# Two of eight expert groups summed on TensorE instead of scattered to memory, in a fused four-block transformer kernel

## The chip, the cores and the metric

One core of a Trainium2 chip runs the whole program. The metric is device time in microseconds (us) of that core for one execution, as the median of several runs. The core has five engines that run side by side, each from its own queue in order: TensorE (PE in the profile; its weight loads are PEld) for matmuls, VectorE (DVE) and ScalarE (ACT) for element work, GpSimd (POOL), which here mostly issues indirect DMAs, and SyncE (SP), which issues the plain DMAs. Engines wait for each other through semaphores. SBUF is the on-chip memory; PSUM is where TensorE writes its products.

## The reference

The reference passes 4096 tokens of 128 features through twelve sublayers: four blocks, each of a half-weighted feed-forward, an attention and the same feed-forward again. The change is in the two feed-forwards of block 1, a mixture of experts:

```python
x = x + 0.5 * _L1_ffn_ref(_layernorm(x), ...)
x = x + _L1_attn_ref(_layernorm(x), ...)
x = x + 0.5 * _L1_ffn_ref(_layernorm(x), ...)

def _moe_forward(x, router_w, w_gate, w_up, w_down, ws_gate_up, ws_down):
    probs = softmax(x @ router_w.T)                  # 64 experts
    topk_w, topk_ids = top_k(probs, 8)
    topk_w = topk_w / sum(topk_w)
    ...                                              # pos: how many earlier tokens chose that expert
    valid = pos < 64                                 # 64 places per expert
    xb = ...                                         # (64 experts, 64 places, 128)
    h = silu(xb @ w_gate) * (xb @ w_up)              # 96 hidden
    y = h @ w_down
    routed = segment_sum(y * topk_w * valid, token)
    shared = silu(x @ ws_gate) * (x @ ws_up) @ ws_down
    return routed + shared
```

The expert takes the first 64 tokens that chose it. With 64 x 64 = 4096 places and 8 choices a token, 512 tokens at the least are needed to fill all places; for the given input the first 1024 tokens fill them. Later tokens get the shared expert alone.

## The kernel before

**Layout.** `x` holds all tokens in SBUF as 32 blocks of 128 tokens; a piece is four blocks (512 tokens), so there are eight pieces. `xn` is the normalised x and `xnT` its transpose, which the matmuls read. `norm_piece(c)` does one piece's layernorm: statistics and an inverse root on VectorE (L305 to L319), then four scalings on ScalarE (L328). `turn_piece(c)` transposes it: four matmuls into `ln_tp` and a copy by ScalarE (L336, L337). All transposes share one PSUM pool, `pst`, with two buffers ("tp"): whoever takes a buffer waits, in the order of the program, until the user before the last has been read.

**Order.** `pin` (L240) chains instructions of one engine in the order in which the program writes them. So the queue of each engine is set by hand in the expert loop; outside of it a scheduler places them.

**Routing.** `ffn1(call, normed)` (L963) handles `FIRST` = 8 blocks (two pieces) in general. `routing` computes logits, a softmax, the best eight of 64 (L1002 to L1031). `slots` (L1038) finds for every expert its first 64 tokens: eight rounds of MAX8 and MATCH_REPLACE8 on VectorE, transposes of the result into lists (L937 to L943), then `idx` and `idy`, the row numbers for the gathers and scatters (L1064, L1065). `f_cp` and `more` (L1080, L1081) count the places that are still empty. The shared expert of the first two pieces follows in the text: `shared_up` (L979), a gate product `sgp`, an up product `sup`, silu and their product `sh`; `shared_down` (L991), a product `yp` (in the PSUM bank of `sgp`) added to x (L996). Then x of these pieces is stored to memory as accumulator `acc[0]` (L234). There are four accumulators in memory in all; the other three start at zero.

Every engine then reads `more` and branches (L1121): only if places were empty does `general()` handle all tokens. For this input the branch is always taken past it.

**Experts.** The 64 experts go in eight groups of eight. For group g: `fetch` (L1134, four indirect gathers on GpSimd), `turn` (L1145), `gates` (L1156, sixteen matmuls, silu on ScalarE L1158), `product` (L1163, `hh` on VectorE), `down` (L1172, products `y`; L1188, VectorE multiplies by the routing weight into `ys`; L1192, four indirect scatter-adds on GpSimd into the accumulators). Sixteen matmuls on a constant (`idle`, L258) go ahead of the first group. In the same loop run the shared expert of the other six pieces, the load of the weights two groups ahead (L1114, L1116), and the layernorm of pieces for what follows. In call 0 that is attention; in call 1 (`normed`) it is block 2, whose experts choose tokens: `pick` (L1426: logits `f_lp`, L1436, L1447) and `best` (L1452: four rounds of MAX8, FIND_INDEX8 and MATCH_REPLACE8 per piece, L1458 to L1464, split in two halves of two rounds).

**End.** A second branch on `more` (L1254) guards the return of the later pieces. In call 0 attention then reads the accumulators of the first two pieces into SBUF (`returned` L1359, with L1363 and L1367) and sums them with three VectorE adds a piece (`summed`, L1370). It begins with other pieces: `project` (a_zp L1278, a_nm L1293). In call 1 `gather_acc` (L946) does the same at once: x from acc[0] (L952), six loads of the other accumulators (L955), six adds (L956), and then `choose` normalises, picks and searches for these two pieces.

Of the kernel before, what the change touches and what calls it, by code (L numbers as in the profile page):

```python
# [9 lines left out]
F32 = mybir.dt.float32  # L10
# [21 lines left out]
NS0 = NB0 * B0 // P  # L32

E1, K1, F1, CAP1 = 64, 8, 96, 64
FIRST = 8
XW = D + E1
GE1 = 8
# [34 lines left out]
def macaron_kernel(ctx: ExitStack, tc: tile.TileContext, I: dict, out: bass.AP):  # L72
# [146 lines left out]
    xl_dram = dram.tile([T + PAD, XW], F32, name="xl_dram")  # L219

    acc_two = [dram.tile([2 * (T + PAD), D], F32, name=f"acc{n}") for n in range(NACC // 2)]
    acc = [a[h * (T + PAD) : (h + 1) * (T + PAD), :] for a in acc_two for h in range(2)]
    SP.dma_start(out=xw_dram[T:, :], in_=zeros[:, :XW])
    SP.dma_start(out=xn_dram[T:, :], in_=zeros[:, :D])
# [114 lines left out]
    def tok(j):  # L339
        return xnT[:, j * P : (j + 1) * P]  # L340
# [618 lines left out]
    piece_order = [FIRST // 4, FIRST // 4 + 1, *range(FIRST // 4), *range(FIRST // 4 + 2, NT // 4)]  # L959
    begun = piece_order[:2]  # L960


    def ffn1(call, normed):  # L963
        pinned.clear()
# [7 lines left out]
        with tc.tile_pool(name=f"f1r{call}", bufs=1) as rp, tc.tile_pool(name=f"f1w{call}", bufs=2) as wp, tc.tile_pool(  # L972
            name=f"f1t{call}", bufs=2
        ) as tp2:
            idx = rp.tile([P, E1 // 2], I32, name="f1_idx")
            idy = rp.tile([P, E1 // 2], I32, name="f1_idy")
            more = rp.tile([1, 1], I32, name="f1_more")
# [60 lines left out]
            def slots(key, n, key_pool):  # L1038

                keyT = key_pool.tile([P, n * P], F32, tag="keyT", name="f1_keyT")  # L1040
                for c in range(0, n, 4):
                    tp = pst.tile([P, 512], F32, tag="tp", name="f1_ktp")
                    for i in range(4):
                        PE.transpose(
                            tp[:, i * P : (i + 1) * P], key[:, c + i, :, :].rearrange("p h e -> p (h e)"), ident
                        )
                    S.copy(keyT[:, c * P : (c + 4) * P], tp)
                first = key_pool.tile([P, CAP1], F32, tag="first", name="f1_first")
                for r in range(CAP1 // 8):
# [12 lines left out]
                for h in range(2):  # L1062
                    rows = slice(h * CAP1, (h + 1) * CAP1)
                    V.tensor_scalar(idx[rows, :], empty[rows, h::2], float(T), None, ALU.add)  # L1064
                    V.tensor_scalar(idy[rows, :], empty[rows, h::2], float(T + h * (T + PAD)), None, ALU.add)  # L1065
                return slot

            with tc.tile_pool(name=f"f1p{call}", bufs=2, space=PSUM) as pr, tc.tile_pool(name=f"f1k{call}", bufs=1) as key_pool:
# [53 lines left out]
                general()  # L1122

            pinned.clear()
            with tc.tile_pool(name=f"f1h{call}", bufs=1, space=PSUM) as ph:
                n, groups, others = GE1 // 2, E1 // GE1, NT // 4 - FIRST // 4
                xgs, turned, hidden, w = {}, {}, {}, early
# [36 lines left out]

                def down(g):
                    wd, (hh, _) = w[g][1], hidden.pop(g)
                    y = ph.tile([P, n, D], F32, tag="y", name="f1_y", bufs=2)
                    for i in range(n):
                        for h in range(2):
                            e = 2 * i + h  # L1170
                            pin(
                                PE.matmul(  # L1172
                                    y[h * CAP1 : (h + 1) * CAP1, i, :],
                                    hh[:, e * CAP1 : (e + 1) * CAP1],
                                    wd[:, e, :],
                                    start=True,
                                    stop=True,
                                    skip_group_check=True,
                                )
                            )  # L1180

                    flat = xgs.pop(g).rearrange("p e w -> p (e w)")
                    ys = tp2.tile([P, n, D], F32, tag="ys", name="f1_ys", bufs=2)
                    for h in range(2):
                        rows = slice(h * CAP1, (h + 1) * CAP1)
                        w0 = D + g * GE1 + h
                        wcol = flat[rows, w0 : w0 + (n - 1) * (XW + 2) + 1 : XW + 2]
                        pin(V.tensor_tensor(ys[rows, :, :], y[rows, :, :], bc(wcol, 2, D), ALU.mult))  # L1188
                    for i in range(n):
                        e = g * n + i  # L1190
                        pin(
                            G.indirect_dma_start(  # L1192
                                out=acc_two[e % 2],
                                out_offset=bass.IndirectOffsetOnAxis(ap=idy[:, e : e + 1], axis=0),
                                in_=ys[:, i, :],
                                in_offset=None,
                                compute_op=ALU.add,
                            )
                        )
# [12 lines left out]
                for g in range(groups):  # L1212
# [41 lines left out]
            with tc.If(rv > 0):  # L1254
                gather_acc(acc, FIRST, NT, add=True)
                if normed:
                    choose(range(FIRST // 4, NT // 4))
                else:
                    for c in begun:
                        norm_piece(c)  # L1260
                        turn_piece(c)
            if normed:
                gather_acc(acc, 0, FIRST, n=4, bufs=6)
                choose(range(FIRST // 4))


    def attn1():

        scale = float(DH) ** -0.5 / D
        with tc.tile_pool(name="a1", bufs=3) as ap, tc.tile_pool(name="a1a", bufs=2, space=PSUM) as pa, tc.tile_pool(  # L1270
# [88 lines left out]
            def returned(c):  # L1359

                rows = slice(4 * c * P, (4 * c + 4) * P)
                xc = x[:, 4 * c : 4 * c + 4, :]
                SP.dma_start(out=xc, in_=acc[0][rows, :].rearrange("(j p) d -> p j d", p=P))  # L1363
                parts[c] = []
                for a in acc[1:]:
                    t = ap.tile([P, 4, D], F32, tag="acc", name="acc_t", bufs=6)
                    SP.dma_start(out=t, in_=a[rows, :].rearrange("(j p) d -> p j d", p=P))  # L1367
                    parts[c].append(t)

            def summed(c):  # L1370
                xc = x[:, 4 * c : 4 * c + 4, :]
                for t in parts.pop(c, []):
                    pin(V.tensor_tensor(xc, xc, t, ALU.add))

            pinned.clear()
            parts = {}
# [9 lines left out]
            for s in range(BATCH + 7):  # L1386
# [12 lines left out]
                    if p < pieces:  # L1399
                        turn_piece(piece_order[p])  # L1400
                if s in ahead:
                    summed(piece_order[ahead[s]])
# [890 lines left out]
```

## Time and profile before

| | |
|---|---|
| median of 8 runs | 2882.48 us (2873.9 to 2893.54) |
| profiled execution, its own time | 2885.66 us |
| span in its trace | 2884.0 us |
| mean granted TensorE clock | 0.859 of full |
| busy: PE / DVE / ACT / POOL | 2343.1 / 1490.7 / 1059.5 / 768.5 us |
| PE share of the chain that ended last | 32% |
| call 0: gates of group 0 to first a_nm of attention | 720.79 to 825.86 us |
| call 1: gates of group 0 to the first scaling after the return | 981.89 to 1134.28 us |
| scatter-adds of both calls (L1192) | 64, mean 1570 ns |

The times are from the start of the span. The granted clock is the share of its full rate at which TensorE was let run in a stretch of time. "SPq", "DVEq" or "PEq" is the part of an engine that handles waits, branches and DMA issues; idle time "<-DVEq L1121" is idle time that ended when that engine had passed the branch of line 1121.

### The profile page before, as it was taken

The page shows a single profiled execution, that of the slowest core. Times are in us where ns is not written, and L with a number is a line of the kernel's source. Part 1 is how long each engine was busy: PE and PEld are TensorE (multiplying, and loading weights), DVE is VectorE, ACT ScalarE, POOL GpSimd, SP SyncE. Part 2 cuts the span into 40 slices and gives each one's busy share as a digit, 9 for nine tenths or more (in the row PEclk, how much of TensorE's full clock was granted, in tenths as well). Part 3 has the DMA queues.
Part 4 walks back from the last instruction along what each step waited for, and adds up shares of the span by engine and source line. Part 5 has one row for each costly group of instructions (what it writes and reads, how often), then busy time and mean ns, then how long its engine had stood idle before and what let it go on. Part 6 is the DMA issues. An engine that isn't in the chain of part 4 may idle for free. (4 is left out here: it accounts for less than half of the span.)

```text
span 2884.0 us, 45798 instructions
## 1 busy us (share of the span) xinstructions
PE 2343.1 (81%) x16869; PEld 1720.2 (60%) x16869; DVE 1490.7 (52%) x4388; ACT 1059.5 (37%) x2388; POOL 768.5 (27%) x695
## 2 busy tenths in 40 slices
PE   6986887993866573477999993786999899999999
PEld 5873555792655452355666662554777655557777
DVE  5446565445557566423345566224555666645553
ACT  1322221231234221243444431443444355663443
POOL 1650000561730352476000102872111100012111
PEclk9997887996779665677999995658999799999999
DMA  5861231563530445356000003552000012220000
GB/s 153 274 163 48 77 104 60 168 180 91 148 69 8 122 106 143 76 148 150 23 5 8 5 8 96 137 140 67 1 1 1 10 49 64 64 66 7 8 8 11
DMA packets 207909, 221.14 MB, mean 77 GB/s; under 512 B 46265, under 2 KB 172938, under 8 KB 204306
## 3 DMA queue, kind: packets, MB, share of 16 engines
q1 hardware_dynamic: 171066, 179.80, 20.3%
q0 software_dynamic: 36608, 38.31, 7.5%
q8 instruction: 136, 2.23, 0.3%
q14 instruction: 99, 0.81, 0.1%
HBM read 145.88 MB, written 63.50 MB: 73 GB/s over the span
## 5 line engine op out<-in xcount | busy, mean ns | idle before, releaser
L328 ACT ACTIVATE xn<-x,ln_less,ln_r 128x128 f32<-128x128 f32 x288 | 118.6, 482 | 380.4 <-DVE ln_less L319 374.6
L871 DVE TENSOR_REDUCE a_nm<-a_s 128x4 f32<-128x1024 f32 x128 | 156.4, 1224 | 102.1 <-PE a_t L867 90.4
L515 PE MATMUL f_h<-f_xsT,f_w 128*128 128x256 f32 x736 | 183.3, 393 | 1.5 <-DVE f_xsT L504 1.4
L1667 PE MATMUL f_h<-f_xgT,f_w 128*128 128x128 f32 x768 | 152.8, 360 | 36.8 <-DVE f_xgT L1661 36.8
L875 ACT ACTIVATE a_e<-a_t 128x512 f32<-128x512 f32 x256 | 139.0, 594 | 98.9 <-PE a_t L867 98.9
L1671 ACT ACTIVATE f_hs<-f_h,w_f_b 128x128 f32<-128x128 f32 x384 | 109.5, 369 | 172.1 <-PE f_h L1667 168.8
L867 PE MATMUL a_t<-a_q,a_k 32*128 32x256 f32 x1024 | 168.3, 412 | 3.5 <-ACT a_e L875 3.3
L1667 PEld LDWEIGHTS f_h<-f_xgT,f_w 128*128 128x128 f32 x768 | 129.7, 255 | 60.8 <-DVE f_xgT L1661 60.8
L1702 POOL DMA_INDIRECT acc<-f_ys,f_idx x96 | 151.9, 1582 | 49.8 <-DVE f_ys L1697 29.3
L518 DVE SCALAR_TENSOR_TENSOR f_hs<-f_h,f_b1s,f_sg 128x256 f32<-128x256 f32 x184 | 88.8, 484 | 141.7 <-ACT f_sg L517 141.7
L867 PE MATMUL a_s<-a_k,a_q 32*128 32x256 f32 x1024 | 155.5, 431 | 2.3 <-DVE a_nm L871 1.6
L517 ACT ACTIVATE f_sg<-f_h,f_b1s 128x256 f32<-128x256 f32 x184 | 87.1, 474 | 170.5 <-PE f_h L515 169.6
L515 PEld LDWEIGHTS f_h<-f_xsT,f_w 128*128 128x128 f32 x736 | 133.7, 196 | 24.0 <-issue 7.6
L336 PE MATMUL ln_tp<-ident,xn 128*128 128x128 f32 x288 | 64.1, 337 | 97.5 <-ACT xn L328 97.2
L1697 DVE TENSOR_SCALAR f_ys<-f_up,f_xg,f_share 128x128 f32<-128x128 f32 x96 | 39.3, 410 | 187.9 <-PE f_up L1694 162.8
L2089 ACT ACTIVATE f_nh<-f_c,w_f_sh 128x256 f32<-128x256 f32 x192 | 87.0, 500 | 127.7 <-DVE f_c L2108 103.2
L489 POOL DMA_INDIRECT f_xs<-xn_dram,f_src x92 | 91.0, 989 | 132.8 <-DVE f_own L458 57.9
L2036 POOL TENSOR_TENSOR f_t<-f_nh 128x512 f32<-128x512 f32 x16 | 20.4, 1273 | 380.7 <-PE f_m L2070 361.1
L867 PEld LDWEIGHTS a_s<-a_k,a_q 32*128 32x128 f32 x1024 | 90.9, 198 | 47.3 <-issue 34.0
L1192 POOL DMA_INDIRECT acc<-f_ys,f_idy x64 | 100.5, 1570 | 64.5 <-DVE f_ys L1188 37.6
L867 PEld LDWEIGHTS a_t<-a_q,a_k 32*128 32x128 f32 x1024 | 104.4, 189 | 17.2 <-ACT a_e L875 12.6
L336 PEld LDWEIGHTS ln_tp<-ident,xn 128*128 128x128 f32 x288 | 40.3, 162 | 124.6 <-ACT xn L328 110.8
(455 smaller groups left out, 5563.1 us busy)
## 6 DMA issues: line engine op xcount, KB each, us to landing
f_w<-in_f_w SPq DMA_DIRECT2D x24, 1024.0 KB
f_w<-in_f_w SPq DMA_DIRECT2D x46, 512.0 KB
f_w<-in_f_w SPq DMA_DIRECT2D x70, 256.0 KB
a_ud<-a_u SPq DMA_DIRECT2D x32, 512.0 KB
f_wgu<-in_f_wgu SPq DMA_DIRECT2D x16, 768.0 KB
acc<-zeros SPq DMA_DIRECT2D x14, 512.0 KB
acc_t<-acc SPq DMA_DIRECT2D x28, 256.0 KB
f_wd<-in_f_wd SPq DMA_DIRECT2D x16, 384.0 KB
```

The lines of the kernel that those rows point to most:

```text
L328: S.activation(xn[:, t0 + j, :], x[:, t0 + j, :], AF.Identity, bias=less[:, j : j + 1], scale=r[:, j : j + 1])
L336: pin(PE.transpose(tp[:, i * P : (i + 1) * P], xn[:, 4 * c + i, :], ident))
L489: G.indirect_dma_start(out=xs[:, i, :], out_offset=None, in_=xn_dram, in_offset=bass.IndirectOffsetOnAxis(ap=src[:, s : s + 1], axis=0),)
L515: pin(PE.matmul(h[:, k, :], w1[:, cc * P : (cc + 1) * P], xsT, start=True, stop=True))
L518: V.scalar_tensor_tensor(hs[:, c, :], h[:, 1, :], b1[:, b, c : c + 1], sg, ALU.add, ALU.mult)
L867: pin(PE.matmul(ps[:, c, :], sta[:, c * P : (c + 1) * P], mov, start=True, stop=True))
L871: pin(V.tensor_reduce(m, sp, AX.X, ALU.max, negate=True))
L875: pin(S.activation(e, tp, AF.Exp, scale=scale))
L1192: G.indirect_dma_start(out=acc_two[e % 2], out_offset=bass.IndirectOffsetOnAxis(ap=idy[:, e : e + 1], axis=0), in_=ys[:, i, :], in_offset= ...
L1667: pin(PE.matmul(h[:, s, :], w1[:, e % GE2, s, :], xgT, start=True, stop=True))
L1671: pin(S.activation(acts[e][:, s, :], h[:, s, :], AF.Gelu, bias=W["f2_b1"][:, col : col + 1]))
L1702: G.indirect_dma_start(out=acc2[e % 2], out_offset=bass.IndirectOffsetOnAxis(ap=idx[:, e : e + 1], axis=0), in_=ys, in_offset=None, comput ...
```

## The change

The outputs `ys` of the last two groups (6 and 7) are no longer scattered. Each group has four lists of 128 places (two experts each), eight lists in all. For each list and each of the two pieces of 512 tokens, VectorE makes a 128x512 matrix that is 1 where a place's token is the column's token (`place`), and TensorE multiplies `ys` of the list, as weights, with it, adding up over the eight lists in two PSUM banks `sums` (`put`): sixteen compares and sixteen 128x512 fp32 matmuls per call. ScalarE copies `sums` over the first 1024 columns of `xnT`, and `summed` transposes them back (four transposes a piece) and adds them to x as one more VectorE add per piece.

To find room in PSUM, `sup` of the shared expert moves from its own bank into the pool of the transposes, and `y` has one buffer instead of two. The token numbers `tokf` cost four small VectorE steps in the routing. A counting row comes from an iota on GpSimd. At most two compares of each piece are kept ready (`bufs=2`), so `place(i + 2)` waits for list i's matmul.

`returned` and `summed` move out of attention and serve both calls. In call 1 the accumulators are read within the loop, at g = 6, with three buffers instead of six, and summed ahead of the second branch. The `ys` of the two groups are also stored to `ys_dram`, so that the branch's body can scatter them when tokens behind the first 1024 have places.

```diff
+SUMMED = 2
...
+    def returned(pool, bufs=3):
+        for c in range(FIRST // 4):
+            rows = slice(4 * c * P, (4 * c + 4) * P)
+            xc = x[:, 4 * c : 4 * c + 4, :]
+            SP.dma_start(out=xc, in_=acc[0][rows, :].rearrange("(j p) d -> p j d", p=P))
+            parts[c] = []
+            for a in acc[1:]:
+                t = pool.tile([P, 4, D], F32, tag="acc", name="acc_t", bufs=bufs)
+                SP.dma_start(out=t, in_=a[rows, :].rearrange("(j p) d -> p j d", p=P))
+                parts[c].append(t)
+    def summed(c):
+        xc = x[:, 4 * c : 4 * c + 4, :]
+        for t in parts.pop(c):
+            pin(V.tensor_tensor(xc, xc, t, ALU.add))
+        tp = pst.tile([P, 512], F32, tag="tp", name="f1_stp")
+        for i in range(4):
+            pin(PE.transpose(tp[:, i * P : (i + 1) * P], tok(4 * c + i), ident))
+        pin(V.tensor_tensor(xc, xc, tp.rearrange("p (j d) -> p j d", d=D), ALU.add))
...
-                sup = pool.tile([F1, 512], F32, tag="su", name="f1_sup", bufs=1)
+                sup = pst.tile([P, 512], F32, tag="tp", name="f1_sup")[:F1, :]
...
+                    for k in range(2):
+                        late = empty[rows, E1 - 2 * tail + h :: 2]
+                        V.tensor_scalar(tokf[rows, k, :], late, float(T - 512 * k), None, ALU.add)
...
+                G.iota(count_up, pattern=[[1, 512]], base=0, channel_multiplier=0, allow_small_or_imprecise_dtypes=True)
+                sums = [ph.tile([P, 512], F32, name=f"f1_sum{k}") for k in range(2)]
+                def place(i):
+                    for k in range(2):
+                        ohs[i, k] = op.tile([P, 512], F32, tag=f"oh{k}", name="f1_oh", bufs=2)
+                        pin(V.tensor_scalar(ohs[i, k], count_up, tokf[:, k, i : i + 1], None, ALU.is_equal))
+                def put(g):
+                    ys = yss.pop(g)
+                    for j in range(n):
+                        i = (g - groups + SUMMED) * n + j
+                        for k in range(2):
+                            pin(PE.matmul(sums[k], ys[:, j, :], ohs.pop((i, k)),
+                                start=i == 0, stop=i == tail - 1, skip_group_check=True))
+                        if i + 2 < tail:
+                            place(i + 2)
...
-                    y = ph.tile([P, n, D], F32, tag="y", name="f1_y", bufs=2)
+                    y = ph.tile([P, n, D], F32, tag="y", name="f1_y", bufs=1)
...
+                    if g >= groups - SUMMED:
+                        late = (g - groups + SUMMED) * n * P
+                        SP.dma_start(out=ys_dram[late : late + n * P, :]..., in_=ys)
+                        yss[g] = ys
+                        return
                     for i in range(n):
                         e = g * n + i
                         pin(G.indirect_dma_start(...))
...
                     if g + 2 < groups:
                         turn(g + 2)
+                    if g == groups - SUMMED - 1:
+                        place(0)
+                        place(1)
+                    if g >= groups - SUMMED:
+                        put(g)
+                    if g == groups - 2 and normed:
+                        returned(op)
                     if other:
                         shared_down(c, ph, sh, pin)
                     if normed and 2 <= g < others + 2:
                         pick(c - 2)
                         best(c - 2, 0, 2)
+                for k in range(2):
+                    pin(S.copy(xnT[:, k * 512 : (k + 1) * 512], sums[k]))
                 if normed:
                     best(first + others - 1, 2)
+                    for c in range(FIRST // 4):
+                        summed(c)
             rv = nc.values_load(more[0:1, 0:1], min_val=0, max_val=P * E1)
             with tc.If(rv > 0):
...
             if normed:
-                gather_acc(acc, 0, FIRST, n=4, bufs=6)
                 choose(range(FIRST // 4))
...
-            for c in range(FIRST // 4):
-                returned(c)
+            returned(ap, 6)
```

The loop's body calls `down(g)` first, then `gates(g + 1)` and `product(g + 1)`, and `put(g)` behind them, so `put(6)` stands between the gates and the down products of group 7, and `put(7)` behind those.

More of the change, by code (lines that the diff above doesn't have):

```diff
@@ L221, in macaron_kernel @@
     acc_two = [dram.tile([2 * (T + PAD), D], F32, name=f"acc{n}") for n in range(NACC // 2)]
+    ys_dram = dram.tile([SUMMED * GE1 // 2 * P, D], F32, name="ys_dram")
     acc = [a[h * (T + PAD) : (h + 1) * (T + PAD), :] for a in acc_two for h in range(2)]
@@ L960, in macaron_kernel @@
     begun = piece_order[:2]
+    parts = {}
+    def returned(pool, bufs=3):
[16 more added lines that the diff above has]
+        pin(V.tensor_tensor(xc, xc, tp.rearrange("p (j d) -> p j d", d=D), ALU.add))
     def ffn1(call, normed):
@@ L976, in ffn1 @@
             idy = rp.tile([P, E1 // 2], I32, name="f1_idy")
+            tail = SUMMED * GE1 // 2
+            tokf = rp.tile([P, 2, tail], F32, name="f1_tokf")
             more = rp.tile([1, 1], I32, name="f1_more")
@@ L1124, in ffn1 @@
             pinned.clear()
-            with tc.tile_pool(name=f"f1h{call}", bufs=1, space=PSUM) as ph:
+            with tc.tile_pool(name=f"f1h{call}", bufs=1, space=PSUM) as ph, tc.tile_pool(
+                name=f"f1o{call}", bufs=1
+            ) as op:
                 n, groups, others = GE1 // 2, E1 // GE1, NT // 4 - FIRST // 4
-                xgs, turned, hidden, w = {}, {}, {}, early
+                xgs, turned, hidden, w, yss, ohs = {}, {}, {}, early, {}, {}
+                count_up = op.tile([P, 512], F32, name="f1_no")
+                G.iota(count_up, pattern=[[1, 512]], base=0, channel_multiplier=0, allow_small_or_imprecise_dtypes=True)
[9 more added lines that the diff above has]
+                        for k in range(2):
+                            pin(
+                                PE.matmul(
+                                    sums[k],
+                                    ys[:, j, :],
+                                    ohs.pop((i, k)),
+                                    start=i == 0,
+                                    stop=i == tail - 1,
+                                    skip_group_check=True,
+                                )
+                            )
+                        if i + 2 < tail:
+                            place(i + 2)
                 def fetch(g):
@@ L1188, in down @@
                         pin(V.tensor_tensor(ys[rows, :, :], y[rows, :, :], bc(wcol, 2, D), ALU.mult))
+                    if g >= groups - SUMMED:
+                        late = (g - groups + SUMMED) * n * P
+                        SP.dma_start(
+                            out=ys_dram[late : late + n * P, :].rearrange("(i p) d -> p i d", p=P), in_=ys
+                        )
+                        yss[g] = ys
+                        return
                     for i in range(n):
@@ L1250, in ffn1 @@
                         best(c - 2, 0, 2)
+                for k in range(2):
+                    pin(S.copy(xnT[:, k * 512 : (k + 1) * 512], sums[k]))
                 if normed:
                     best(first + others - 1, 2)
+                    for c in range(FIRST // 4):
+                        summed(c)
             rv = nc.values_load(more[0:1, 0:1], min_val=0, max_val=P * E1)
             with tc.If(rv > 0):
+                with tc.tile_pool(name=f"f1s{call}", bufs=2) as sp2:
+                    behind = sp2.tile([P, tail], F32, name="f1_behind", bufs=1)
+                    V.tensor_scalar(behind, tokf[:, 0, :], float(FIRST * P), None, ALU.is_ge)
+                    for i in range(tail):
+                        ys = sp2.tile([P, D], F32, tag="ys", name="f1_gys")
+                        SP.dma_start(out=ys, in_=ys_dram[i * P : (i + 1) * P, :])
+                        V.tensor_scalar(ys, ys, behind[:, i : i + 1], None, ALU.mult)
+                        e = E1 // 2 - tail + i
+                        G.indirect_dma_start(
+                            out=acc_two[e % 2],
+                            out_offset=bass.IndirectOffsetOnAxis(ap=idy[:, e : e + 1], axis=0),
+                            in_=ys,
+                            in_offset=None,
+                            compute_op=ALU.add,
+                        )
                 gather_acc(acc, FIRST, NT, add=True)
@@ L1357, in norm @@
                 G.tensor_tensor(xc, xc, bc(W["a1_bo"], 1, 4), ALU.add)
[L1359 to L1373, printed above, removed]
             pinned.clear()
-            parts = {}
-            for c in range(FIRST // 4):
-                returned(c)
+            returned(ap, 6)
             for c in begun:
@@ L1401, in attn1 @@
                 if s in ahead:
-                    summed(piece_order[ahead[s]])
+                    if piece_order[ahead[s]] < FIRST // 4:
+                        summed(piece_order[ahead[s]])
                     norm(piece_order[ahead[s]])
```

## The prediction

> **What bounds the kernel now.** I read the page first. Its chain of waits that ended last gives TensorE 32% and leaves most of the span to short steps on all engines, so no single engine sets the time. The change touches two stretches of some 150 us (the two calls of the MoE sublayer of block 1), and I read those in the timeline, engine by engine. Columns: start, duration, engine, operation, and in brackets the idle time before it with what ended it.
>
> The place where both calls go from routing to the experts, here in call 0:
>
> ```profile
> 684.98 0.69 DVE L996 SCALAR_TENSOR_TENSOR x<-f_yp,x 128x512 f32<-128x512 f32 x1 [1.25 <-PE f_yp L994]
> 708.13 0.19 PE L1080 MATMUL f_cp<-ones,f_count 128*1 128x1 f32 x2 [1.41 <-DVE f_count L1078]
> 708.47 0.15 DVE L1081 CAST f_more<-f_cp 1x1 int32<-1x1 f32 x1
> 710.01 5.28 PE L258 MATMUL idle<-carry_on,ident 128*128 128x256 f32 x16 [1.69 <-PEq L1121]
> 712.50 0.87 DVE L305 BATCH_NORM_STATS2 ln_st<-x 128x6 f32<-128x128 f32 x4 [3.89 <-DVEq L1121]
> 720.79 1.54 PE L1156 MATMUL f_hg<-f_xgT,f_wgu 128*96 128x64 f32 x8 [0.68 <-ACT f_xgT L1147]
> ```
>
> The shared expert (L996) is over 23 us before the count of empty slots (L1080). After the cast, TensorE and VectorE go straight to the branch (L1121), which costs 1.69 and 3.89 us of idle time. Gates of group 0 start at 720.79.
>
> The end of call 0, and how attention begins:
>
> ```profile
> 820.60 1.56 POOL L1192 DMA_INDIRECT acc<-f_ys,f_idy  x1 [0.30 <-issue]
> 821.94 0.38 SPq L1363 DMA_DIRECT2D x<-acc  x1
> 825.86 0.69 DVE L1293 TENSOR_REDUCE a_nm<-a_zp 128x4 f32<-128x512 f32 x1 [11.12 <-SPq L1254]
> ```
>
> VectorE stands for 11.12 us until the last scatter-add (820.60) has landed. The change removes the two last groups' scatters, on which this wait ends. The end of call 1:
>
> ```profile
> 1109.75 1.56 POOL L1192 DMA_INDIRECT acc<-f_ys,f_idy  x1 [0.30 <-issue]
> 1112.55 0.24 DVE L1464 TENSOR_SCALAR f_kv<-f_kv,base 128x32 f32<-128x32 f32 x1
> 1122.18 3.38 SPq L955 DMA_DIRECT2D acc_t<-acc  x6
> 1125.59 1.42 DVE L956 TENSOR_TENSOR x<-x,acc_t 128x512 f32<-128x512 f32 x2 [12.80 <-DMA acc_t<-acc]
> 1134.28 1.65 ACT L328 ACTIVATE xn<-x,ln_less,ln_r 128x128 f32<-128x128 f32 x4 [28.27 <-DVE ln_less L319]
> ```
>
> The top-32 search (L1464) ends at 1112.79, the accumulators return at 1125.59, and the next normalisation starts at 1134.28. In the windows (PE, PEld, DVE, ACT, POOL busy, granted clock, DMA share, GB/s) the stretch before that wait is not idle:
>
> ```profile
> 1085.00:1113.00 28.00, 15.02 (x96) 12.01 (x96) 23.02 (x86) 5.11 (x13) 12.46 (x8) 0.62 0.26 34
> 1095.00:1106.00 11.00, 8.99 (x44) 6.45 (x44) 9.31 (x31) 2.97 (x8) 3.36 (x3) 0.52 0.22 37
> 801.00:815.00 14.00, 9.37 (x80) 8.05 (x79) 7.42 (x27) 3.30 (x7) 8.44 (x6) 0.78 0.31 29
> ```
>
> VectorE is 82% busy in call 1's last 28 us, TensorE 82% in eleven of them at a clock of 0.52. So the gap of 12.80 us is a gap after a full stretch, and the new work is put into that stretch.
>
> **Prices.** One new product is a 128x512 fp32 matmul, two records. The nearest row is the shared expert's (L985): 1.02 us a pair at full clock (757.47), 1.91 at half (748.52). At the clocks above (0.78, 0.52 to 0.62) I take 1.3 us; bounds 1.02 and 1.95. One new compare is a 128x512 tensor_scalar:
>
> ```profile
> L1753 DVE TENSOR_SCALAR a_spread<-ones,rowm 128x64 f32<-128x64 f32 x4 | 1.0, 248 | 0.1
> L1559 DVE TENSOR_SCALAR f_taken<-f_cv,f_lim 128x256 f32<-128x256 f32 x2 | 0.7, 343 | 0.0
> L956 DVE TENSOR_TENSOR x<-x,acc_t 128x512 f32<-128x512 f32 x22 | 15.1, 687 | 33.6 <-DMA acc_t<-acc 33.4
> ```
>
> From 64 to 256 columns 95 ns, so 0.495 ns a column, and 343 + 256 x 0.495 = 470 ns at 512; the bound above is the tensor_tensor of that size, 687. Eight scatters (1.56 + 0.30 each, 14.9 us of POOL a call) go away; their wait is priced below.
>
> **Step 1, the count reaches the branch later (both calls).** The second half of the shared expert's first product (f_sup) moves into the two-buffer pool of the transposes. In program order its turn there comes after f_ktp, the lists' f_tp and f_cp, so sup of both pieces, the downs, and two silus and their VectorE steps now stand between the cast and the branch, one after another, because sgp and yp share one bank.
>
> Call 0. What leaves the routing gains: the Exp table load waited for the second silu (681.54) and floor's Ln ran at 686.30; without the downs' matmuls between the transposes the first can be at 682.25, 4.0 earlier. Four small tokf steps cost 0.35 before the cast, which ends at 708.62 - 4.0 + 0.35 = 705.0. Then in series, at half clock after 12 us of idle TensorE: sup0 2.1 (from 704.4), sh0 0.7, sup1 beside it to 708.5, yp0 1.5, x0 0.8, sgp1 2.0, silu1 0.7, sh1 0.7, yp1 1.8, x1 0.8: VectorE is free at 716.8. The branch, 3.9, to 720.7; the normalisation that stands between L305 and the first xn, 4.0; xn 1.65; f_xgT copy 0.6: gates start at 727.1 instead of 720.79, **+6.3** (bounds +3 if the products run warm, +9 if the 4.0 isn't gained). The first fetches on POOL need only idx, so they are there by then; POOL idles 1.68 us before its first scatter now, so a shift of gates beyond that shifts POOL's chain too.
>
> Call 1. No gain: four xn on ACT (1.65) now come between Exp and Ln, +1.1, less the 0.67 of x1 that stood there: +0.4. Cast 970.9, the same chain: yp1 ends at 982.4; branch 1.5; the idle matmuls (5.85 at 971.70 now) to 989.7; four transposes 1.1, copy 0.6: gates at 991.4 instead of 981.89, **+9.5** (bounds +6, +12).
>
> **Step 2, the end of call 0.** Gates of group 7 end at 807.8. put(6): lists 0 and 1, four products, 5.2, to 813.0; lists 2 and 3 need compares that stand behind hh(7) (ends 811.7) and are in time: to 818.2. down(7), which started at 811.75, is queued behind: to 819.7; ys(7) to 821.1; put(7), 10.4, to 831.5; TensorE's branch 0.7 (its row at L1254), a_zp 2.2: a_nm at 834.4 instead of 825.86, **+8.5**. The wait of 11.12 is gone, but TensorE is behind by more. At 1.02 a product it is +5, at 1.95 +19; below it stands +2, if the first four hide. Two further adds of 0.69 in attention lie in VectorE's idle fifth (18.81 busy of 24 us at 826 to 850); uncovered they would cost 1.4.
>
> **Step 3, the end of call 1.** put(6): lists 0 and 1 in TensorE's idle time after 1091.0. Compares 2 and 3 stand on VectorE behind hh(7) and two rounds of the search, so they start at 1099.6; lists 2 and 3 run from 1100.5 to 1105.7. The next search's logits (f_lp) are behind them: to 1108.7, copy 0.4, so its two rounds start at 1109.1, not 1099.60, and end at 1112.0; ys(7) to 1113.4; two rounds to 1116.3. put(7): lists 4 and 5 to 1118.6, 6 and 7 to 1123.8. The last f_lp 3.0 and copy 0.4: four rounds of search 1127.2 to 1133.2 instead of 1106.80 to 1112.79. Now the accumulators are there, the 12.80 is gone; piece 0's four adds 2.8, piece 1's three tiles are loaded only when those adds free their buffers (landing 3.4 after issue, as 1122.18 to 1125.59), so 3.4 more: 1139.4. The branch of VectorE, hidden in the wait before, 3.9 by L1121's row (0.7 by TensorE's at L1254); normalisation 4.0: xn at 1147.3 instead of 1134.28, **+13.0** (+10 at 1.02, +20 at 1.95; 0 if searches and products overlap fully).
>
> Edits at nothing: the iota (0.65 by its 128x128 row of 0.263) lies under the branch chain; the 0.5 MB of stores on SP have no reader; one y buffer instead of two is free when down needs it, since ys follows y at once (uncovered 1.4 a group, ys' two halves); f_sup's turn among the transposes inside the loop falls behind their copies (uncovered 0.7 a piece, L988).
>
> **Sum.** 6.3 + 9.5 + 8.5 + 13.0 = 37.3 on the profiled execution's 2885.7: 2923. That execution is 3.2 over the median of the runs, so **2920**; all other stretches are as before.
>
> [...] The windows' clocks of 0.52 to 0.78 speak for the slower product, above all where products wait for compares. [...]
>
> **Rivals.**
> - Cold products (0.12). All at 1.95: 6.3 + 9.5 + 19 + 20 = 55, 2938. For: clock 0.52 in 1095 to 1106. Against: 0.78 in call 0.
> - The routing chain is hidden (0.15). Steps 1 cost nothing, because POOL's fetches and the branch would have to be waited for anyway: 8.5 + 13.0 = 21.5, 2904. For: fetches end at 719.8. Against: gates start one copy after the last transpose already.
> - The tails cancel (0.13): removed waits pay for the products, step 1 alone, 15.8: 2898.
> - The gaps close (other side, 0.10). Products fit TensorE's idle time (13 us in 1085 to 1113) and compares VectorE's 5: call 1 gains 12.8 less branch 3.9 and two adds 1.4 = 7.5, call 0 its 11.1 less two copies of 0.59 and a_zp 2.0 = 7.9. With step 1 it is 15.4 against 15.8, 2882, not slower (0.07); with step 1 hidden as well 2867 (0.03). It decides if the eight late products of a call, with the compares they wait for, cost under 11 us. Against: 16 products need 16 to 31 us.
>
> **How the numbers follow.** The forecast has 0.5: 2920, its own range 2905 to 2936. 0.3% (8.6 us) is what a measurement can tell from no change, so slower is over 2891: 0.5 + 0.12 + 0.15 + 0.13 = 0.90; within 0.07; faster 0.03. From 2892 to 2940 all four slower cases are held, less their edges.
>
> **What would show it.** Right: f_sup, the downs and two silus between the cast and L1121; gates of group 0 some 6 and 9 us later after the cast's place; a_nm without a wait for the scatter but after the products; the search of call 1 ending some 20 us later, adds directly behind it without a wait of 12.80. Wrong: products at 1.0 us tucked into idle time, the searches not delayed, f_sup done before the keys' transposes.

## The result, and the profile after

The changed kernel takes 2919.28 us (median of 17 runs, 2912.99 to 2931.45) against 2885.82 us of the kernel before (46 runs), a ratio of 1.0124, 95% interval 1.0106 to 1.0141. It is 33 us slower; 2920 was forecast. Its profiled execution has a span of 2924.8 us.

Seven lines of TensorE, VectorE and POOL from the timeline of the changed kernel show the way from routing to the experts in call 0:

```profile
697.71 0.19 PE L1112 MATMUL f_cp<-ones,f_count 128*1 128x1 f32 x2 [1.41 <-DVE f_count L1110]
697.82 3.73 PE L1014 MATMUL f_sup<-xnT,w_f_sgu 128*96 128x512 f32 x4
706.54 1.94 PE L1023 MATMUL f_yp<-w_f_sd,f_sh 96*128 96x128 f32 x8 [1.40 <-DVE f_sh L1017]
713.64 0.87 DVE L307 BATCH_NORM_STATS2 ln_st<-x 128x6 f32<-128x128 f32 x4 [4.43 <-DVEq L1153]
713.87 0.56 POOL L1163 IOTA f_no<- 128x512 f32 x1 [66.50 <-DVEq L1153]
715.14 0.99 POOL L1196 DMA_INDIRECT f_xg<-xw_dram,f_idx  x1 [0.71 <-issue]
722.76 2.83 PE L1218 MATMUL f_hg<-f_xgT,f_wgu 128*96 128x64 f32 x16 [0.68 <-ACT f_xgT L1209]
```

f_sup now starts behind f_cp, and both pieces of the shared expert run one after the other until 708.5. Only then do VectorE and POOL pass the branch. The gates start 25.1 us behind f_cp; before it was 12.7 (708.13 to 720.79).

The end of call 0, from the same timeline. The last line answers to the a_nm of before, which waited 11.12 us:

```profile
808.64 3.65 PE L1179 MATMUL f_sum<-f_oh,f_ys 128*128 128x512 f32 x8
814.06 3.70 PE L1179 MATMUL f_sum<-f_oh,f_ys 128*128 128x512 f32 x8 [1.77 <-DVE f_oh L1171]
820.28 7.13 PE L1179 MATMUL f_sum<-f_oh,f_ys 128*128 128x512 f32 x16 [0.91 <-DVE f_ys L1250]
829.38 0.69 DVE L1388 TENSOR_REDUCE a_nm<-a_zp 128x4 f32<-128x512 f32 x1 [4.87 <-PE a_zp L1375]
```

Two records make one product: 7.13 us for eight is 0.89 us each. The wait for the scatter is gone, and the products put somewhat more time in its place.

The end of call 1:

```profile
1115.81 5.40 PE L1179 MATMUL f_sum<-f_oh,f_ys 128*128 128x512 f32 x8 [4.82 <-DVE f_oh L1171]
1127.62 9.98 PE L1179 MATMUL f_sum<-f_oh,f_ys 128*128 128x512 f32 x16 [3.18 <-DVE f_ys L1250]
1137.54 0.65 PE L1514 MATMUL f_lp<-xnT,w_f_rw 128*64 128x256 f32 x4
1139.67 0.43 DVE L1536 MAX8 f_cv<-f_lg 128x8 f32<-128x256 f32 x1 [4.97 <-ACT f_lg L1527]
1145.58 2.13 DVE L982 TENSOR_TENSOR x<-x,acc_t 128x512 f32<-128x512 f32 x3
1156.68 0.25 DVE L1831 TENSOR_SCALAR a_spread<-ones,rowm 128x64 f32<-128x64 f32 x1 [4.00 <-DVEq L1335]
1163.40 1.65 ACT L330 ACTIVATE xn<-x,ln_less,ln_r 128x128 f32<-128x128 f32 x4 [22.52 <-DVE ln_less L321]
```

The adds (1145.58) follow the search with no wait; the 12.80 us of before is gone. But the search itself starts late: f_lp (1137.54) had stood behind the eight products of put(7), and VectorE idled 4.97 us for it. The windows of these ends (same columns as before) go with the two prices of a product. The first row is the kernel before in call 0, the other two are the changed kernel in call 0 and call 1:

```profile
801.00:829.00 28.00, 16.45 (x105) 13.75 (x105) 9.20 (x32) 6.95 (x19) 17.17 (x12) 0.70 0.35 49
801.00:829.00 28.00, 24.19 (x124) 13.49 (x123) 15.55 (x45) 5.53 (x11) 4.06 (x4) 0.98 0.18 37
1098.00:1142.00 44.00, 34.37 (x148) 20.11 (x144) 25.59 (x87) 6.11 (x15) 0.54 (x4) 0.79 0.16 52
```

The clock was 0.98 in call 0 and 0.79 in call 1. In the same 28 us of call 0 the kernel before had 0.70, with TensorE busy for 16.5 us in place of 24.2, of which the products are 14.5: here the higher clock goes with the denser work. In call 1 the last twelve products come in two runs, and the clock changes within each:

```profile
1115.81:1119.70 3.89, 3.89 (x5) 1.63 (x6) 2.11 (x5) 0.00 (x0) 0.00 (x0) 0.57 0.00 0
1119.76:1124.20 4.44, 4.44 (x36) 2.82 (x34) 1.87 (x5) 0.65 (x2) 0.00 (x0) 1.00 0.00 0
1127.62:1132.90 5.28, 5.28 (x7) 2.18 (x7) 3.61 (x12) 0.00 (x0) 0.00 (x0) 0.50 0.17 50
1132.90:1137.50 4.60, 4.60 (x11) 1.86 (x9) 0.97 (x2) 0.00 (x0) 0.00 (x0) 0.95 0.00 0
```

TensorE had idled 4.82 us for a compare ahead of the first run and 3.18 us for ys ahead of the second. Each run begins at about half the clock, 0.85 us from one record to the next, and after 3.9 and 5.3 us goes on at nearly full clock with 0.43 us. The first four products of call 1, close behind the gates, take 0.91 each. So the mean of the sixteen is 1.19 us in call 1 and 0.91 in call 0.

### The profile page after: what moved, and what is told of

The parts are those of the page before. It is cut to its first block, busy times and chain, and to the rows that moved or that the text cites. A ratio compares the mean times of both kernels' runs of the same rounds, so it can differ in the third digit from the quotient of the medians.

```text
span 2924.8 us, 46046 instructions
## 1 busy us (share of the span) xinstructions
PE 2392.6 (82%) x16949; PEld 1742.9 (60%) x16949; DVE 1509.6 (52%) x4432; ACT 1065.2 (36%) x2394; POOL 744.1 (25%) x681
## 5 line engine op out<-in xcount | busy, mean ns | idle before, releaser
L1780 POOL DMA_INDIRECT acc<-f_ys,f_idx x96 | 151.9, 1582 | 51.9 <-DVE f_ys L1775 30.0
L517 PEld LDWEIGHTS f_h<-f_xsT,f_w 128*128 128x128 f32 x736 | 132.7, 195 | 24.1 <-issue 7.6
L1775 DVE TENSOR_SCALAR f_ys<-f_up,f_xg,f_share 128x128 f32<-128x128 f32 x96 | 39.3, 410 | 196.5 <-PE f_up L1772 156.1
L338 PEld LDWEIGHTS ln_tp<-ident,xn 128*128 128x128 f32 x288 | 39.9, 161 | 119.7 <-ACT xn L330 106.3
L538 POOL DMA_INDIRECT yt_dram<-f_ys,f_dst x92 | 91.0, 990 | 67.3 <-DVE f_ys L534 52.1
```

Source lines behind the costliest of these rows:

```text
L338: pin(PE.transpose(tp[:, i * P : (i + 1) * P], xn[:, 4 * c + i, :], ident))
L517: pin(PE.matmul(h[:, k, :], w1[:, cc * P : (cc + 1) * P], xsT, start=True, stop=True))
L538: G.indirect_dma_start(out=yt_dram, out_offset=bass.IndirectOffsetOnAxis(ap=dst[:, s : s + 1], axis=0), in_=ys[:, i, :], in_offset=None,)
L1780: G.indirect_dma_start(out=acc2[e % 2], out_offset=bass.IndirectOffsetOnAxis(ap=idx[:, e : e + 1], axis=0), in_=ys, in_offset=None, comput ...
```

## The experiments

Times of one kernel on different chips differ: on the chips of the experiments the kernel before took some 2945 us in place of 2886. So each run has its ratio to the kernel before of its own batch, and four stretches are read from each trace by the timeline:

- start 0: from the last sum of block 0 (L569 before) to the gates of group 0, call 0
- start 1: from the last attention add (L1352 before) to the gates of group 0, call 1
- end 0: from the end of the gates of group 7 to the first a_nm
- end 1: from the end of the gates of group 7 to the first xn after the return

| kernel | start 0 | start 1 | end 0 | end 1 | ratio, 95% interval |
|---|---|---|---|---|---|
| before, first trace | 52.8 | 41.3 | 18.1 | 43.3 | |
| after, first trace | 60.6 | 50.8 | 20.6 | 55.9 | 1.0124 (1.0106 to 1.0141) |
| c_before | 52.4 | 40.9 | 19.3 | 41.3 | single run |
| c_after | 60.9 | 51.2 | 19.6 | 52.8 | 1.0136 (1.0114 to 1.0158) |
| p1_bank_alone | 58.9 | 51.1 | 19.0 | 38.7 | 1.0071 (1.0043 to 1.0099) |
| e1_own_bank | 52.2 | 39.9 | 20.6 | 53.9 | 1.0065 (1.0037 to 1.0093) |
| e2_iota_first | 60.9 | 51.9 | 20.7 | 54.1 | 1.0082 (1.0050 to 1.0114) |
| e3_few_products | 61.8 | 49.6 | 17.3 | 48.1 | 1.0086 (1.0057 to 1.0115) |
| e4_few_compares | 58.8 | 49.7 | 18.5 | 46.6 | 1.0067 (1.0042 to 1.0093) |
| e5_pool_compares | 50.9 | 40.2 | 23.8 | 49.0 | 1.0061 (1.0039 to 1.0084) |
| e6_behind_search | 53.2 | 40.1 | 20.6 | 47.2 | 1.0036 (1.0006 to 1.0065) |
| b1_early_loads | 52.6 | 39.3 | 16.2 | 38.5 | 1.0004 (0.9988 to 1.0019) |
| b2_kept_ys | 52.4 | 40.8 | 11.4 | 39.1 | 1.0011 (0.9993 to 1.0029) |
| b3_both | 52.2 | 40.7 | 11.7 | 37.8 | 0.9980 (0.9959 to 1.0001) |

e1 to e4 ran in one batch; c_after, e5, b1 and b2 in a second on the same chip; c_before, e6 and b3 in a third on another chip; p1 alone on one more. Kernels with the same code for a stretch differ by up to 3 us in it, and by 4.6 in end 1 of the kernel before (38.7 to 43.3 in four traces): smaller differences aren't read.

> The changed kernel again, as the control of this chip: 1.2% over the kernel before (interval of the result 1.0106 to 1.0141), gates 25 and 21 us behind f_cp, first scaling after the return 56 us behind the gates of group 7.

The control was met but for end 1, which is 3 us shorter than in the first trace.

**Own bank.** e1 undoes the move of f_sup in the routing; p1 makes that move alone in the kernel before.

```diff
-def shared_up(c, pool, keep=lambda ins: ins):
+def shared_up(c, pool, keep=lambda ins: ins, own=False):
...
-    sup = pst.tile([P, 512], F32, tag="tp", name="f1_sup")[:F1, :]
+    if own:
+        sup = pool.tile([F1, 512], F32, tag="su", name="f1_sup", bufs=1)
+    else:
+        sup = pst.tile([P, 512], F32, tag="tp", name="f1_sup")[:F1, :]
...
-    shared_down(c, pr, shared_up(c, pr))
+    shared_down(c, pr, shared_up(c, pr, own=True))
```

> The changed kernel, but in the routing f_sup has a PSUM bank of its own again (inside the expert loop it stays in the transposes' pool). Theory (the shared expert, pushed behind the count of empty places, makes the experts start late): the gates of group 0 start 14 us after f_cp in call 0 and 13 in call 1 (changed kernel 25.0 and 20.7, before 12.7 and 11.8; some 1.3 of the rest is the iota), and the time falls by 15 us to about 2904. Rival (the delay is POOL's own: its branch around a larger body, the iota, the gathers): the gates stay over 20 us behind f_cp and the time within 5 us of the changed kernel's. Rival (all of the loss is in the two ends): the gates move, but the loop takes it up and the time stays at 2919.

The f_cp and the gates of both calls in e1's timeline:

```profile
734.90 0.19 PE L1115 MATMUL f_cp<-ones,f_count 128*1 128x1 f32 x2 [1.41 <-DVE f_count L1113]
748.76 2.83 PE L1221 MATMUL f_hg<-f_xgT,f_wgu 128*96 128x64 f32 x16 [0.68 <-issue]
1010.66 0.19 PE L1115 MATMUL f_cp<-ones,f_count 128*1 128x1 f32 x2 [1.41 <-DVE f_count L1113]
1021.29 1.57 PE L1221 MATMUL f_hg<-f_xgT,f_wgu 128*96 128x64 f32 x16 [0.68 <-ACT f_xgT L1212]
```

The gates start 13.9 and 10.6 us behind f_cp instead of 25 and 21, and both starts are those of the kernel before.

```diff
-    sup = pool.tile([F1, 512], F32, tag="su", name="f1_sup", bufs=1)
+    sup = pst.tile([P, 512], F32, tag="tp", name="f1_sup")[:F1, :]
```

> The kernel before with one line of the change alone: f_sup takes its buffer from the transposes' pool, in the routing and in the loop. All groups are scattered, nothing is summed on TensorE. Theory (this line makes the experts start late, some 20 us in both calls, and nothing later takes it up): gates 24 and 21 us behind f_cp, less 0.6 and 0.3 for the iota that isn't there, the ends as before (18 to 19 and 41 to 43 us behind the gates of group 7), 1.0065 of the kernel before. Rival (the late start is waited for anyway where POOL's scatters end each call): 1.002 or less.

Call 0 in p1's timeline:

```profile
733.95 0.19 PE L1080 MATMUL f_cp<-ones,f_count 128*1 128x1 f32 x2 [1.41 <-DVE f_count L1078]
734.07 3.41 PE L985 MATMUL f_sup<-xnT,w_f_sgu 128*96 128x512 f32 x4
756.45 2.83 PE L1156 MATMUL f_hg<-f_xgT,f_wgu 128*96 128x64 f32 x16 [0.68 <-issue]
```

f_sup stands behind f_cp as in the changed kernel, and the gates start 22.5 us behind f_cp in call 0 and 20.9 in call 1. The starts are late by 6 and 10 us, the ends aren't, and this line alone costs 0.71%. The numbers of the theory were met within some 2.5 us; the rivals (POOL's own delay, a late start that is waited for anyway) fall. So about half of the loss (0.71% of 1.24 to 1.36%, by intervals that are wide) has nothing to do with the summing itself: it is the room that the summing's PSUM banks took. The four stretches show 14 us of the 21 that 0.71% is; a part of the rest is told under the sum of the steps.

**Iota.** It is moved behind the gathers of the first three groups.

```diff
-    G.iota(count_up, pattern=[[1, 512]], base=0, ...)
...
     for g in range(3):
         fetch(g)
+    pin(G.iota(count_up, pattern=[[1, 512]], base=0, ...))
```

> The changed kernel, but the iota stands behind the gathers of the first three groups on POOL, not ahead of them. Theory (gates wait for POOL's gathers, so the iota ahead of them is on the path): gates 1.2 us nearer to f_cp in each call (23.8 and 19.5), 2917 in all, which only the trace can tell. Rival (my prediction's step: VectorE's normalisation and the idle matmuls decide, the iota is free): 25.0 and 20.7 as before.

In no trace do the gates start earlier or later than 7.4 to 7.7 us behind the first gather, before and after: the gather is the last link. But the gather came only 0.7 and 0.3 us sooner behind TensorE's own passing of the branch (5.7 and 2.1 us, c_after 6.4 and 2.4), and the starts of 60.9 and 51.9 don't show it. The expected 1.2 was too much. The gates start 24.6 and 21.8 us behind f_cp: these are the rival's numbers (25.0 and 20.7, no gain) and not the theory's (23.8 and 19.5). The ratio is lower than c_after's, yet the medians are 2976.7 and 2982.1 us with runs that overlap; no gain is shown.

**Products and compares.** In e3 TensorE leaves out twelve products a call, in e4 VectorE twelve compares.

```diff
 # e3
+    oh = ohs.pop((i, k))
+    if 0 < i < tail - 1:
+        continue
 # e4
-    ohs.pop((i, k)),
+    ohs[i % 2, k],
...
-    if i + 2 < tail:
-        place(i + 2)
```

> The changed kernel without twelve of the sixteen f_sum products of each call: only the first and the last of the eight lists are summed; all compares stay. Theory (the products delay what is queued behind them on TensorE: down and f_lp of group 7): a_nm comes 8 us earlier after the gates of group 7, the last search of call 1 starts 11 us earlier, in all 19 us: 2900. Rival (the compares on VectorE are the price of both ends): under 5 us.

> The changed kernel without twelve of the sixteen compares of each call: all lists are multiplied with the one-hot matrices of the first two. Theory (products wait for compares that stand behind VectorE's search): call 0 gains the 1.8 us that put(6) waits, call 1 some 5, since lists 2 and 3 run directly behind the gates: 2912. Rival (products alone): no more than 2 us. Rival (compares alone): more than 12 us.

Against 52.8 to 54.1 us of the three kernels with the same end 1 (c_after, e1, e2), e3 has 48.1 and e4 46.6: about 5 and 7 us. Against their end 0 of 19.6 to 20.7, e3 has 17.3 and e4 18.5. So e3 was expected at 11 and 8 and gave half or less; e4 was expected at 5 and gave more. Their ratios are 0.50% and 0.69% below c_after's, where 0.65% and 0.24% were expected. Neither resource alone is the price. The edits fit this account: each product waits for a compare and each compare (with two buffers) for a product, and both stand in queues that the searches share; taking one away leaves the other's queue.

> The changed kernel with f_sup's own bank in the routing, and the products (with the compares that they call for) of groups 6 and 7 behind pick and the half search of their step instead of ahead of them. Theory (products stand ahead of f_lp on TensorE and so make the searches late): from the gates of group 7 to the first scaling 49 us (54 with the bank alone), 1.005 of the kernel before. Rival (VectorE's total work sets the end, the order of TensorE does nothing): 53 us or more.

```diff
-    if g >= groups - SUMMED:
-        put(g)
     if g == groups - 2 and normed:
         returned(op)
...
         best(c - 2, 0, 2)
+    if g >= groups - SUMMED:
+        put(g)
```

With the own bank of e1 and the products behind pick and the half search, end 1 is 47.2 instead of 53.9: with all products and compares kept, the place of put was worth 6.7 us of this stretch. The edit moves the products in TensorE's queue and the compares that they call for in VectorE's, so it is the place in both queues. The last search ends 27.9 us behind the gates instead of 35.6; then 4.3 us are waited for the loads of piece 1. The rival (VectorE's total decides) falls by these traces, one of each kernel, on two chips. A gain in the whole time isn't shown: 1.0036 and 1.0065 have intervals that overlap.

> The changed kernel with f_sup's own bank in the routing, and the sixteen compares of each call on POOL instead of VectorE. Theory (in call 1 the compares cost twice: they lengthen VectorE's full queue, and products wait for them behind the search): from the gates of group 7 to the first scaling 46 us as without the compares (changed kernel 55.9), and 0.3% below the 1.0065 of the own bank alone. Rival (POOL's compare takes 1.3 us as its 128x512 steps do, and the products now wait for POOL): 54 us or more.

The edit is `G.tensor_scalar` for `V.tensor_scalar` in place, on top of e1. POOL's row in its timeline:

```profile
836.27 6.75 POOL L1174 TENSOR_SCALAR f_oh<-f_no,f_tokf 128x512 f32<-128x512 f32 x4
```

It takes 1.69 us a compare, where VectorE needs 0.49. End 1 gains 5 us, end 0 loses 3 (23.8): 1.0061 against 1.0065, no gain that can be told, where 0.3% was expected. Its end 1 of 49.0 lies between the theory's 46 and the rival's 54.

**The waits of the kernel before.** Two kernels ask what they were made of, without summing anything on TensorE.

```diff
 # b1
+    late = ExitStack()
+    op = late.enter_context(tc.tile_pool(name=f"f1a{call}", bufs=1)) if normed else None
...
     if normed:
         best(first + others - 1, 2)
+        back = {}
+        rows = slice(0, FIRST * P)
+        SP.dma_start(out=x[:, :FIRST, :], in_=acc[0][rows, :].rearrange("(j p) d -> p j d", p=P))
+        for k, a in enumerate(acc[1:]):
+            t = op.tile([P, FIRST, D], F32, tag="acc", name="acc_t", bufs=3)
+            SP.dma_start(out=t, in_=a[rows, :].rearrange("(j p) d -> p j d", p=P))
+            for c in range(FIRST // 4):
+                back[c, k] = t[:, 4 * c : 4 * c + 4, :]
...
-    gather_acc(acc, 0, FIRST, n=4, bufs=6)
+    for (c, k), t in sorted(back.items(), key=lambda kv: kv[0]):
+        xc = x[:, 4 * c : 4 * c + 4, :]
+        V.tensor_tensor(xc, xc, t, ALU.add)
+    late.close()
 # b2: kept is a pool that is opened ahead of call 0 and closed behind attn1
-    idy = rp.tile([P, E1 // 2], I32, name="f1_idy")
+    idy = (kept or rp).tile([P, E1 // 2], I32, name="f1_idy")
...
-    ys = tp2.tile([P, n, D], F32, tag="ys", name="f1_ys", bufs=2)
+    ys = (kept or tp2).tile([P, n, D], F32, tag="ys", name="f1_ys", bufs=2)
```

> The kernel before, for its trace on this chip: the same stretches as on the first chip, gates 12.7 and 11.8 us behind f_cp, a_nm 18 us behind the gates of group 7, the first scaling of call 1 43 us behind them; the loop between, which takes 96 to 99 and 123 us in all traces of this chip instead of 87 and 109, as long as in the others.

> The kernel before (all eight groups scattered), but in call 1 the accumulators get buffers of their own in the expert loop and are loaded ahead of the second branch, four loads instead of eight; the adds stay behind it. Theory (of the wait of 12.80 only some 4 us is the last scatter's landing and the load; the rest is the loads' own wait behind the branch and a 1 MB weight load, since their buffers are fresh memory): the wait falls to about 5 us and the time by 7 us, 0.25%. Rival (the wait is the scatter's landing): it stays at 11 us or more and so does the time.

The first adds in c_before and, in a second fence, in b1:

```profile
1186.38 1.42 DVE L956 TENSOR_TENSOR x<-x,acc_t 128x512 f32<-128x512 f32 x2 [11.94 <-DMA acc_t<-acc]
```

```profile
1169.30 1.29 DVE L1275 TENSOR_TENSOR x<-x,acc_t 128x512 f32<-128x512 f32 x2 [5.61 <-DVEq L1264]
1172.91 1.29 DVE L1275 TENSOR_TENSOR x<-x,acc_t 128x512 f32<-128x512 f32 x2 [2.31 <-DMA acc_t<-acc]
```

The first wait is 5.61, and the profile puts it down to VectorE's branch instead of a load; 2.31 more is waited for the next load. In four traces with the old end the first wait is 9.93 to 12.80 (10.18 in b2, of the same batch). All waits among the adds are 10.6 to 13.3 us there and 8.3 in b1, so 2 to 5 us went. The edit changed the place of the loads, their number and their buffers at once, and it isn't shown which of these did it. The 7 us that were expected don't come: end 1 is 38.5, where four traces with the old end have 38.7 to 43.3, and the ratio is 1.0004.

> The kernel before, but in call 0 ys and idy lie in a pool that is kept until the end of the attention. Theory (the attention's first step waits for the last scatter only because its buffers take over the memory that the scatter still reads; no data of the scatter is needed so early): a_nm starts when POOL has issued the last scatter, 3 us earlier than before (15 us behind the gates of group 7 instead of 18.1), 0.1%, which only the trace can tell. Rival (data or the branch hold it): 18 us.

The a_nm lines of c_before, and of b2 with the step behind it:

```profile
873.71 0.69 DVE L1293 TENSOR_REDUCE a_nm<-a_zp 128x4 f32<-128x512 f32 x1 [10.98 <-SPq L1254]
```

```profile
868.12 0.69 DVE L1293 TENSOR_REDUCE a_nm<-a_zp 128x4 f32<-128x512 f32 x1 [5.96 <-POOLq L1253]
868.85 3.26 DVE L1294 TENSOR_TENSOR a_nm<-a_nm 128x1 f32<-128x1 f32 x1
869.01 3.07 POOL L1381 TENSOR_TENSOR x<-x,w_a_bo 128x512 f32<-128x512 f32 x2
```

End 0 is 11.4, where the traces with the old end have 16.2 to 19.3 (15 was expected): for these 5 to 8 us attention waited for memory that the scatter still read, not for its data. Some 3 us are lost in the step behind it (last section), and attention as a whole takes 117.6 us in b2 and 116.4 in b3, against 114.5 to 115.0. The ratio of 1.0011 shows no gain.

> The kernel before with both edits, early loads in call 1 and the kept ys in call 0. Theory (both waits shorten and the gains add: 4.8 and 6.7 us in the traces of the two alone, less 2 that attention gives back): 9 us, 0.997 of the kernel before. Rival (what is gained is waited for again further on, as the single times of 1.0004 and 1.0011 say): 1.000.

b3 has both short ends (11.7 and 37.8) and a ratio of 0.9980. Its interval ends at 1.0001, so that it is faster than the kernel before is likely and not certain; against the changed kernel it is about 1.5% faster, by the ratios of two batches. Neither edit alone could be told from the kernel before by its time.

## Why the prediction was right

**Step 1, call 0: +6.3 forecast, +7.7 measured** (52.8 to 60.6). The gain ahead of the branch was right (4.7 us from L569 to f_ktp, 4.0 forecast), and so was the chain to the branch: ln_st 15.9 us behind f_cp, 16.2 forecast. The link after it was wrong. I let the normalisation, xn and a copy lead to the gates and took the gathers for done; the gathers stand behind the same branch, on POOL, and the gates follow the first of them by 7.5 us in both kernels. The claim that the fetches "are there by then" failed, at a price of 2.7 us: from ln_st to the gates the sum has 6.4 us and the changed kernel 9.12. The lines of the kernel before had shown it, with 8.29 us (712.50 to 720.79). The iota, priced at nothing, is at most a small part of it: e2 moved it, and the gathers came 0.7 us sooner.

**Step 1, call 1: +9.5 forecast, +9.5 measured** (41.3 to 50.8), by parts that err against each other: +1.6 ahead of f_ktp (0.4 forecast), -0.9 from there to f_cp, +8.9 behind it. Within the last part, too, errors cancel: TensorE passes the branch 10.8 us behind f_cp (some 13.4 in the sum), and the gates come 9.9 us later (7.5 in the sum, 10.2 in the kernel before). Here as well the gathers are the last link. That the part sums agree is luck.

**Step 2: +8.5 forecast, +2.5 measured** (18.1 to 20.6). The chain is the one forecast: a_nm waits for a_zp, which stands behind the products. The mis-sized term is the product, 1.3 us in the sum and 0.89 to 0.93 in the trace; sixteen times 0.4 us is the 6 us that are missing. I took the clock of the window before (0.78 from 801 to 815) for the window after, and there it was 0.98. The lower bound of 1.02 gave +5. In call 1 the clock was 0.57 and 0.50 behind 4.82 and 3.18 us of idle time, and 1.00 and 0.95 a few microseconds later. With the bound of 1.02 a product at both ends the sum is 6.3 + 9.5 + 5 + 10 = 30.8, nearer to the measured 32.3 than the 37.3 that the prediction chose.

**Step 3: +13.0 forecast, +12.6 measured** (43.3 to 55.9), by parts that err against each other. The search ended 38.2 us behind the gates, 4 earlier than forecast: the products took 1.19 us in the mean (1.3 forecast), 0.91 the first four and 1.35 and 1.25 the others. Branch 4.00 (3.9), adds with the late loads 7.1 (6.2); of the 6.2, 3.4 were a wait for loads, and piece 1's adds had no time, while the trace has 1.3 us of waits and 2.8 of adds for that piece. The normalisation took 6.7 instead of 4.0. In it VectorE idles 2.57 us ahead of a second a_spread, a step of the next sublayer, and the profile names nothing that it waits for; the cause is open. A compare took 0.49 us (0.47 forecast from two rows), and 0.39 to 0.45 from one start to the next where several stand in a row.

The loops between are -0.9 and +2.4 us in the first traces and of no fixed sign on the chips of the experiments. The attention behind call 0 takes 116.0 us after 115.0 in the first traces, and 114.3 after 114.5 in c_after and c_before, so that the two further adds have no cost clear of the spread. The sum of the four steps is 32.3 us where 37.3 was forecast, beside 33.5 between the medians. So the forecast of 2920 owes its closeness partly to the kernel before: its median over 46 runs is 3.3 us above that of the eight runs shown.

Nor do the four steps account for all of the time. The two profiled spans differ by 40.8 us: the changed kernel is 5.8 us shorter ahead of start 0 and 11.7 us longer behind end 1, in code that is the same. Some 10 of these lie in the attention of block 3, where the changed kernel has a clock of 0.53 from 2605 to 2630 us, though TensorE is busy for 24.1 of the 25 us; the kernel before has 1.00 in that attention. The same drop is in the traces of c_after, p1, e1, e2, e3, e5 and e6, and not in those of c_before, e4, b1, b2 and b3, one execution each. Whether it comes of the change or comes and goes by execution wasn't tried. So "all other stretches are as before" isn't shown, some 10 us of the difference stay open, and that 32.3 lies so near to 33.5, and 2920 to 2919, is partly luck.

The rival "the tails cancel" holds half: call 0's end does nearly, call 1's doesn't. "The routing chain is hidden" falls by e1 and p1. "Cold products" falls by the 0.91 and 1.19 us of a product, where it has 1.95, and "the gaps close" by both ends, which grew.

## What to carry to other kernels

A buffer that moves to another pool brings that pool's order with it: look which steps stand ahead of it in the new rotation, and what stands behind (here a branch, and behind the branch POOL's gathers). Before a transfer is replaced by arithmetic, ask what its wait consists of: here 5 to 8 us of call 0's wait was memory that the next stage took over, and 2 to 5 us of call 1's went with another place and number of the loads. A few lines took that away without any new work, though the time shows no sure gain (0.9980, interval up to 1.0001). New work on two engines that hand buffers to each other is priced as one chain in the queues that it joins, and its place in them can be worth as much as its amount (e6 against e3 and e4 in end 1).

## What the runs showed of the hardware

- A VectorE step of 128x1 took 3.26 us (0.16 in the kernel before) while POOL ran two 128x512 steps, 3.07 us in all, on the attention's x; it ended with them. b3 repeats it: 3.01 us, ended with POOL's steps. What ties VectorE's step to POOL's wasn't tried.
- The same 128x512 compare takes 0.49 us on VectorE and 1.69 on POOL.
- In call 1 the granted clock of TensorE was 0.57 and 0.50 for 3.9 and 5.3 us after it had idled 4.82 and 3.18 us, and 1.00 and 0.95 behind that; an idle time of 1.77 us in call 0 (814.06) was followed by 1.00 from 814.00 to 817.80.
- In block 3's attention the granted clock was 0.53 from 2605 to 2630 us in the changed kernel, with TensorE busy for 24.1 of the 25 us; eight of fourteen traces have this drop, and the other six don't. The cause is open.
- In all traces of the experiments, on three chips, ACT and VectorE stand still together, ACT for some 5 us (4.8 to 5.3 in c_before), twice in each expert loop, put down to "remote" by the profile; in the first trace of the kernel before no such line is there. The loops take 96 to 99 and 122 to 126 us there instead of 87 and 109. What it is wasn't tried.
